# A pair-update block on one Trainium2 core: where the second layer norm's statistics are made, and what the gate of the output stage is made from

## The chip, the cores and the metric

The kernel runs on one core of a Trainium2 chip. The core has a matrix engine (TensorE, "PE" in the profile, with its weight loads shown apart as "PEld"), a vector engine (VectorE, "DVE"), an activation engine (ScalarE, "ACT"), a general engine (GpSimd, "POOL"), and an engine that here only issues transfers (SyncE, "SP"). The engines work through their own instruction queues in order and wait for one another by semaphores. Data moves between the main memory and the on-chip memory (SBUF) by 16 DMA engines; TensorE writes its products to a second on-chip memory (PSUM). All data is 32-bit floating point.

The metric is the device time of one execution in microseconds. Unless it is said otherwise, a time below is from one profiled execution.

## The reference

The input x is an image of 256 by 256 positions with 128 channels. Four layers follow one another, each of the form x = x + f(groupnorm(x)), where the group norm takes its statistics over all positions and over groups of four channels. The change concerns the third layer (a triangle update) and the hand-over to the fourth (a 3 by 3 convolution). Cut to what matters, the third layer computes:

```python
pair_norm = layer_norm(groupnorm(x2))                 # over the 128 channels, each position
p = pair_norm @ p_in.T ;  g = sigmoid(pair_norm @ g_in.T)
left, right = g[..., :H] * p[..., :H], g[..., H:] * p[..., H:]
out = einsum('bikd,bjkd->bijd', left, right / 256)    # for each channel d a product of 256 x 256 matrices
out = layer_norm(out)                                 # the second norm, over the 128 channels again
out = out @ p_out.T
gate = sigmoid(pair_norm @ g_out.T)
x3 = x2 + gate * out
```

The fourth layer begins with groupnorm(x3), so it needs the sum and the sum of squares of x3 for each channel before it can start.

## The kernel before, in words

The four layers run one after another. Between them the image lies in main memory, channel by channel: x2T, x3T, znT (the first norm's output) and prodD (the 128 products) are arrays of 128 channels by 65536 positions. The third layer is the method `triangle`, and has three stages.

**First stage** (lines 1198 to 1285, the loop with an order of steps written out by hand). It works through 32 pieces of 2048 positions. For each it loads x2T (`ld`), takes the mean over channels with small matrix products whose result lies in four groups of 32 partitions (`mn`, `vr`, the helper `four`), spreads such a row back over all partitions with another small product (`spreads`, which gives `mb` and `pr`), forms the reciprocal root `rs` with Ln and Exp on ScalarE, normalises (`zn`), stores the result to znT (`sto`), and makes a quarter of the factors left and right (`fill`). In the list `order`, a pair (step, lag) means that in turn `it` the step works on piece `it - lag`.

**Second stage** (lines 1287 to 1316). The channels are handled in G = 4 groups of CQ = 32. For each group after the first, znT is read again (tile `zt`, in a ring of five buffers, loaded by SP) and the factors of the group are made (tile `z` in PSUM, 64 blocks, a sigmoid on ScalarE and a multiplication on VectorE into the tile `LR`). Then follow 32 channels: four products into `po` in PSUM, two copies by ScalarE that scale and reorder it into `o` (a ring of three), and a store to prodD that GpSimd issues.

**Third stage** (lines 1322 to 1414, called the output stage below). Again 32 pieces of 2048 positions, two halves of 1024 each. `load` fetches prodD, znT and x2T on SP's queue. `mean` and `centre` subtract the mean over channels from the product, `root` makes the reciprocal root of the variance (with a change of ScalarE's table), `scale` applies it, `gates` makes sigmoid(we * znT), `output` makes the last product `py`, multiplies with the gate on VectorE and adds x2 on GpSimd. `stats` then takes the statistics of x3 on VectorE (bn_stats), and GpSimd issues the store to x3T. After 28 pieces `early_statistics` sums up what there is so far. The order is that of the loop's lines; all of it is pinned to the program's order with `pin`.

After the third stage the method `convolution` calls `group_affine`, which reads the statistics (`mean_variance`), and begins with its products `m`.

Most instructions are issued through helpers, so that the profile gives the helper's line: L61 is every matrix product, L55 every ScalarE activation, L1136 is the line that wraps matrix, VectorE and GpSimd instructions of `triangle`. They are told apart by the names of their tiles.

Of the kernel before, what the change touches and what calls it, by code (L numbers as in the profile page):

```python
# [17 lines left out]
P = 128  # L18
# [13 lines left out]
class Kernel:  # L32
# [78 lines left out]
    def mean_variance(self, pool, stats, tag, shift):  # L111

        nc = self.nc
        mv = pool.tile([P, 2], F32, name=f"mv{tag}")
        if shift is None:

            e, e8 = self.early[tag]
            last, dd = (pool.tile([P, 2], F32, name=f"{n}{tag}") for n in ("ml", "md"))
            nc.vector.bn_aggr(last, stats[:, NCH * 7 // 8:])
            nc.vector.scalar_tensor_tensor(mv, last, 0.125, e8, ALU.mult, ALU.add)  # L120
            nc.vector.tensor_tensor(dd[:, 0:1], e[:, 0:1], last[:, 0:1], ALU.subtract)
            nc.vector.scalar_tensor_tensor(dd[:, 1:2], dd[:, 0:1], 7 / 64, dd[:, 0:1], ALU.mult, ALU.mult)
            nc.vector.tensor_tensor(mv[:, 1:2], mv[:, 1:2], dd[:, 1:2], ALU.add)
        else:

            nc.vector.tensor_reduce(mv, stats, AX.X, ALU.add)
            nc.vector.tensor_scalar_mul(mv, mv, 1.0 / NPIX)
            e = pool.tile([P, 2], F32, name=f"me{tag}")
            nc.vector.tensor_tensor(e[:, 0:1], mv[:, 0:1], shift, ALU.add)
            nc.vector.tensor_tensor(e[:, 1:2], e[:, 0:1], e[:, 0:1], ALU.mult)  # L130
            nc.vector.tensor_tensor(mv[:, 1:2], mv[:, 1:2], e[:, 1:2], ALU.subtract)
        return mv

    def early_statistics(self, stats, tag):

        nc, pin = self.nc, self.tc.keep_in_program_order
        e, e8 = self.early[tag]
        pin(nc.vector.bn_aggr(e, stats[:, :NCH * 7 // 8]))
        pin(nc.vector.tensor_scalar_mul(e8, e, 0.875))
# [989 lines left out]
    def triangle(self, x2T, x3T, znT, prodD, stats2, shift2, stats3, prepare):  # L1129
# [12 lines left out]
        with ExitStack() as c:  # L1142
            wp = c.enter_context(self.pool(name="tw", bufs=1))
            with self.pool(name="twp", bufs=2, space=PSUM) as ps0:
                ab = self.group_affine(wp, ps0, stats2, self.g4, "2", shift=shift2, busy=11)
# [12 lines left out]
                V.tensor_scalar_mul(wo, oraw, low)  # L1158
# [8 lines left out]
            zp = quarters.enter_context(self.pool(name="tz", bufs=5))  # L1167
# [27 lines left out]
            with ExitStack() as c1:  # L1195

                LR = c1.enter_context(self.pool(name="tl", bufs=1)).tile([P, 2, 2, 2 * CQ, P], F32, name="LR")
                with ExitStack() as c2:
# [20 lines left out]
                    def ld(d):  # L1219
                        d["x"] = zp.tile([P, 2048], F32, name="zn", tag="zt")  # L1220
                        nc.sync.dma_start(d["x"], x2T[:, d["p"] * 2048:(d["p"] + 1) * 2048])
# [25 lines left out]
                    def pr(d): d["pr"] = spreads(ps, d["rs"])  # L1247

# [10 lines left out]
                    def fill(k):  # L1259
# [17 lines left out]
                     (ld, 0), (mn, 0), (pr, 2), (zn, 2), (af, 2), (f3, 3), (f1, 3), (mc, 0), (s3, 3), (t3, 3),  # L1277
# [12 lines left out]
                table(SIGMOID)  # L1290
                for g in range(G):

                    for b in range(NB if g else 0):
                        if b % 2 == 0:
                            zt = zp.tile([P, 2048], F32, name="zt", tag="zt")
                            nc.sync.dma_start(zt, znT[:, b * 1024:(b + 2) * 1024])
                        z = ps.tile([P, 8, P], F32, name="z", bufs=3)
# [9 lines left out]
                    for d in range(CQ):  # L1307
                        po = ps.tile([P, 2, 2, P], F32, name="po")
                        for a in range(2):
                            for kc in range(2):  # L1310
                                mm(po[:, a], LR[:, a, kc, d, :], LR[:, :, kc, CQ + d, :], start=kc == 0, stop=kc == 1)
                        o = io.tile([P, 2, P, 2], F32, name="o")
                        for a in range(2):
                            act(o[:, a], po[:, a].rearrange("p b j -> p j b"), AF.Copy, scale=1.0 / N)
                        nc.gpsimd.dma_start(prodD[g * CQ + d].rearrange("(p a j) -> p a j", p=P, a=2),  # L1315
                                            o.rearrange("p a j b -> p a (j b)"))

# [4 lines left out]
            with ExitStack() as c1:  # L1322
                io = c1.enter_context(self.pool(name="t3", bufs=3))
                work = c1.enter_context(self.pool(name="t3w", bufs=2))
# [372 lines left out]
```

## Time and profile before

| What | Value |
|---|---|
| time before, median of 3 runs | 4766.66 us (4765.46 to 4775.34) |
| the profiled execution's own time | 4772.24 us |
| its span, first to last instruction | 4770.2 us |
| mean granted TensorE clock in it | 0.992 of full speed |
| TensorE busy over the span | 4587.0 us, 96% |
| VectorE, ScalarE, GpSimd busy | 3641.1, 3390.9, 2012.0 us |
| DMA packets moved | 801.67 MB, mean 168 GB/s |

The table is to be read with care: busy shares are means over four layers with different limits. Every duration that is used below comes from the profiled execution, whose own time is 5.6 us above the median of the runs. The stages of the third layer are told apart in it by time from the span's start: the first stage up to about 3270 us, the second up to 3841, the output stage up to about 4241, then the convolution.

### The profile page before, as it was taken

The page shows a single profiled execution, that of the slowest core. Times are in us where ns is not written, and L with a number is a line of the kernel's source. Part 1 is how long each engine was busy: PE and PEld are TensorE (multiplying, and loading weights), DVE is VectorE, ACT ScalarE, POOL GpSimd, SP SyncE. Part 2 cuts the span into 40 slices and gives each one's busy share as a digit, 9 for nine tenths or more (in the row PEclk, how much of TensorE's full clock was granted, in tenths as well). Part 3 has the DMA queues.
Part 4 walks back from the last instruction along what each step waited for, and adds up shares of the span by engine and source line. Part 5 has one row for each costly group of instructions (what it writes and reads, how often), then busy time and mean ns, then how long its engine had stood idle before and what let it go on. Part 6 is the DMA issues. An engine that isn't in the chain of part 4 may idle for free.

```text
span 4770.2 us, 79683 instructions
## 1 busy us (share of the span) xinstructions
PE 4587.0 (96%) x30927; PEld 2608.0 (55%) x30927; DVE 3641.1 (76%) x4617; ACT 3390.9 (71%) x5135; POOL 2012.0 (42%) x1356
## 2 busy tenths in 40 slices
PE   8999999999999999999999997899999999999999
PEld 2444555555555433333333332557999943369999
DVE  6776777777777699999999998783533458899886
ACT  6555888888888799999999998895333367742110
POOL 0343555555555456676766666332011024420000
PEclk9999999999999999999999999999999999999999
DMA  8893122222222245555555554665866689954332
GB/s 303 302 347 135 46 89 84 81 86 84 85 81 89 77 94 134 132 132 131 135 132 131 134 132 109 243 257 213 280 241 223 224 311 385 367 211 166 127 121 72
DMA packets 216568, 801.67 MB, mean 168 GB/s; under 512 B 58646, under 2 KB 61996, under 8 KB 171748
## 3 DMA queue, kind: packets, MB, share of 16 engines
q1 hardware_dynamic: 140014, 464.64, 29.1%
q0 software_dynamic: 74880, 331.50, 23.4%
q8 instruction: 248, 4.06, 0.4%
q14 instruction: 130, 1.06, 0.1%
q10 hardware_dynamic: 1296, 0.40, 0.0%
HBM read 464.29 MB, written 265.03 MB: 153 GB/s over the span
## 4 chain that ended last, share of the span: by engine, by line
PE 65%; ACT 14%; DVE 10%; issue 6%; DMA 2%; POOL 2%; SPq 0%; ACTq 0%; POOLq 0%; DVEq 0%
PE z L61 10%; PE m L61 8%; PE nd L61 7%; PE sc L61 6%; PE po L61 5%; PE pr L61 3%; PE ppq L61 3%; PE ppv L61 3%; PE zc L61 2%; PE pe L61 2%; PE py L61 2%; PE ppg L61 2%; PE ppk L61 2%; PE px L61 2%; ACT L950 2%
## 5 line engine op out<-in xcount | busy, mean ns | idle before, releaser
L609 DVE TENSOR_TENSOR e<-sc,bT 128x1024 f32<-128x1024 f32 x512 | 613.5, 1219 | 255.6 <-PE sc L61 253.5
L609 POOL TENSOR_TENSOR ks<-e 128x1024 f32<-128x1024 f32 x256 | 602.0, 2370 | 442.3 <-PE nd L61 428.9
L55 ACT ACTIVATE e<-e 128x1024 f32<-128x1024 f32 x512 | 539.3, 1053 | 39.5 <-DVE e L609 29.9
L1136 DVE TENSOR_TENSOR LR<-z,sg 128x512 f32<-128x512 f32 (+1 forms) x320 | 269.4, 873 | 336.3 <-ACT sg L55 336.3
L61 PE MATMUL m<-U,v 128*128 128x128 f32 x4608 | 514.7, 275 | 0.0
L61 PEld LDWEIGHTS m<-U,v 128*128 128x128 f32 x4608 | 514.6, 192 | 0.0
L61 PEld LDWEIGHTS z<-wf,zt 128*128 128x128 f32 x3072 | 343.5, 192 | 0.2
L61 PE MATMUL z<-wf,zt 128*128 128x128 f32 x3072 | 343.5, 275 | 0.0
L55 ACT ACTIVATE sg<-z 128x512 f32<-128x512 f32 (+1 forms) x320 | 160.6, 512 | 244.6 <-PE z L61 244.3
L61 PE MATMUL sc<-proj 32*128 32x256 f32 x4096 | 300.2, 403 | 3.0 <-DVE e L609 2.1
L978 POOL TENSOR_TENSOR fs<-f 128x512 f32<-128x512 f32 x64 | 175.2, 2737 | 270.1 <-DVE f L975 250.6
L1315 POOL DMA_DIRECT2D prodD<-o x128 | 69.3, 542 | 508.8 <-ACT o L55 499.1
L61 PEld LDWEIGHTS sc<-proj 32*128 32x128 f32 x4096 | 188.1, 185 | 160.8 <-PE px L61 94.8
L61 PE MATMUL nd<-e,proj 128*32 128x256 f32 x4096 | 272.3, 383 | 2.6 <-DVE og L609 2.6
L55 ACT ACTIVATE dn<-dn 128x512 f32<-128x512 f32 x384 | 237.9, 619 | 10.3 <-DVE dn L609 6.2
L978 POOL TENSOR_TENSOR u<-t,tr 128x512 f32<-128x512 f32 x64 | 238.2, 3721 | 11.0 <-DVE tr L981 9.7
L1136 POOL TENSOR_TENSOR xin<-ga,xin 128x1024 f32<-128x1024 f32 x62 | 145.6, 2365 | 213.7 <-DVE ga L1136 213.7
L978 POOL TENSOR_TENSOR t<-t,v 128x1024 f32<-128x1024 f32 x64 | 210.1, 3283 | 59.3 <-DVE t L975 59.3
L61 PE MATMUL po<-LR 128*128 128x256 f32 x1024 | 222.3, 380 | 7.2 <-DVE LR L1136 6.3
L1573 ACT COPY m4s<-m 128x512 f32<-128x512 f32 x32 | 18.7, 583 | 287.1 <-PE m L61 287.1
L1583 POOL DMA_DIRECT2D out_dram<-ys x32 | 37.0, 1156 | 423.9 <-DVE ys L1581 423.9
L61 PEld LDWEIGHTS po<-LR 128*128 128x128 f32 x1024 | 194.1, 190 | 34.6 <-DVE LR L1136 7.1
(392 smaller groups left out, 10986.0 us busy)
## 6 DMA issues: line engine op xcount, KB each, us to landing
zt<-znT SPq DMA_DIRECT2D x96, 1024.0 KB
znT<-zn POOLq DMA_DIRECT2D x61, 1024.0 KB, 6.2
xin<-in_x_dram SPq DMA_DIRECT2D x48, 1024.0 KB
xr<-x3T SPq DMA_DIRECT2D x46, 768.0 KB
x1T<-x POOLq DMA_DIRECT2D x64, 512.0 KB, 4.9
xf<-x1T SPq DMA_DIRECT2D x64, 512.0 KB
xc<-x1T SPq DMA_DIRECT2D x128, 256.0 KB
xc<-t POOLq DMA_DIRECT2D x64, 512.0 KB, 4.7
```

The source lines that it names most:

```text
L55: return self.nc.scalar.activation(out, in_, func, bias=bias, scale=scale, **kw)
L61: return self.nc.tensor.matmul(out, lhsT, rhs, start=start, stop=stop)
L609: pin = lambda f: lambda *a, **k: tc.keep_in_program_order(f(*a, **k))
L950: pin(nc.scalar.preload_act_table_set(want))
L978: pin(nc.gpsimd.tensor_tensor(out, a, b_, op))
L1136: pin = lambda f: lambda *a, **k: tc.keep_in_program_order(f(*a, **k))
L1315: nc.gpsimd.dma_start(prodD[g * CQ + d].rearrange("(p a j) -> p a j", p=P, a=2), o.rearrange("p a j b -> p a (j b)"))
L1573: nc.scalar.copy(m4, m[4])
L1583: nc.gpsimd.dma_start(out[row:row + 8].rearrange("r p t c -> p (r t) c"), ys.rearrange("p g k t c -> p (g k t) c"))
```

## The change

The second norm's mean is no longer taken from the data. The output matrix is multiplied with the centring matrix ahead of the loops, which subtracts the mean over channels in the product itself. The second norm's variance is summed up in the second stage: for each channel, VectorE subtracts a shift (the first channel's product) from `po` and adds the difference to `total`; ScalarE squares the difference; GpSimd adds three of four squares to `even`, VectorE the fourth to `odd`. At the end of the stage the reciprocal root is made once, in a tile of 128 x 512, and written to main memory as rs3D, a single row of 65536 values. The first norm's root is written in the first stage to a like row rs2D (step `sr`). The ring of five buffers `zt` becomes five fixed tiles X[0] to X[4]; the factors use four of them, X[4] holds the sums. `po` moves to the ring of `z` tiles in PSUM, which has four instead of three.

In the output stage the rows rs2D and rs3D are read back (`roots`: one partition of each group of 32 holds 512 positions of each of four pieces) and spread over all partitions by a product with a row of ones (`pa`, `pb`). The gate is made from x2: (x2 - mean) times the first norm's root (`xs`), multiplied with a matrix that holds the group norm's scale and the centring (`wec`). znT is no longer read here. The statistics of x3 come from accumulators: the sum from the multiplication with the gate (`gy`), the sum of squares from a square on ScalarE (`qu`). The loop has a written order with lags, and four PSUM tiles of 1024 instead of three and two of 512.

The diff, cut to its core (small weights made ahead of the loops, the convolution's use of the new statistics, and renamings are left out):

```diff
+                    def sr(d):
+                        for k in range(4):
+                            o = d["p"] * 2048 + k * 512
+                            nc.sync.dma_start(rs2D[:, o:o + 512], d["rs"][32 * k:32 * k + 1])
...
-                     (ld, 0), (mn, 0), (pr, 2), ...
+                     (ld, 0), (sr, 2), (mn, 0), (pr, 2), ...
...
+                shift, total, even, odd = (X[4][:, k * 512:(k + 1) * 512] for k in range(4))
+                nc.gpsimd.memset(X[4][:, 512:], 0.0)
+                squared = []
+                def add_square():
+                    if squared:
+                        n, t = squared.pop()
+                        act(t, t, AF.Square)
+                        if n % 4:
+                            pin(nc.gpsimd.tensor_tensor)(even, even, t, ADD)
+                        else:
+                            tt(odd, odd, t, ADD)
...
-                            zt = zp.tile([P, 2048], F32, name="zt", tag="zt")
+                            zt = X[b // 2 % 4]
-                        z = ps.tile([P, 8, P], F32, name="z", bufs=3)
+                        z = ps.tile([P, 8, P], F32, name="z", bufs=4)
...
-                        po = ps.tile([P, 2, 2, P], F32, name="po")
+                        po = ps.tile([P, 8, P], F32, name="z", bufs=4)[:, :4]
...
                         nc.gpsimd.dma_start(prodD[g * CQ + d]...)
+                        add_square()
+                        if g + d == 0:
+                            act(shift, po.rearrange("p k j -> p (k j)"), AF.Copy, scale=1.0 / N)
+                        else:
+                            df = io.tile([P, 512], F32, name="df", bufs=3)
+                            stt(df, po.rearrange("p k j -> p (k j)"), 1.0 / N, shift, MUL, ALU.subtract)
+                            tt(total, total, df, ADD)
+                            squared.append((g * CQ + d, df))
+                add_square()
+                tt(even, even, odd, ADD)
+                stt(total, total, -1.0 / P, total, MUL, MUL)
+                tt(even, even, total, ADD)
+                table(LN_EXP)
+                act(even, even, AF.Ln, bias=self.eps, scale=1.0 / P)
+                rsm = io.tile([P, 2, P, 2], F32, name="o")
+                for a in range(2):
+                    act(rsm[:, a], even[..half a..], AF.Exp, scale=-0.5)
+                nc.sync.dma_start(rs3D[0].rearrange("(p n) -> p n", p=P), rsm...)
...
+                def roots(b, name, src, queue=nc.sync):
+                    if b * 4 < M:
+                        R[name, b] = io.tile([P, 4, 512], F32, name=name)
+                        v = src[0].rearrange("(p k n) -> k p n", k=4, n=512)
+                        for k in range(4):
+                            queue.dma_start(R[name, b][32 * k:32 * k + 1], v[k:k + 1, 4 * b:4 * b + 4])
+                def spread_of(d, name):
+                    b, j = divmod(d["p"], 4)
+                    d[name] = [ps.tile([P, 1024], F32, name=name, tag="w") for _ in range(2)]
+                    for k in range(4):
+                        mm(d[name][k // 2][:, (k % 2) * 512:(k % 2 + 1) * 512], ones[32 * k:32 * k + 1], R[name, b][32 * k:32 * k + 1, j])
+                def lx(d):
+                    if d["p"] % 4 == 0:
+                        roots(d["p"] // 4 + 1, "ra", rs2D)
+                    load_x(d)
+                def lp(d):
+                    if d["p"] % 4 == 2:
+                        roots(d["p"] // 4 + 1, "rb", rs3D)
+                    load_pd(d)
+                def pa(d): spread_of(d, "ra")
+                def xs(d):
+                    d["xs"] = io.tile([P, 2048], F32, name="xs", bufs=2)
+                    for h in range(2):
+                        stt(half(d["xs"], h), half(d["x"], h), shift3, d["ra"][h], ADD, MUL)
+                def e0(d): product(d, "pe", 0, wec, "xs")
+                def e1(d): product(d, "pe", 1, wec, "xs")
+                def sg(d): ...  act(half(d["ga"], h), d["pe", h], AF.Sigmoid, bias=wbe)
+                def pb(d): spread_of(d, "rb")
+                def sc(d): ...  tt(half(d["pd"], h), half(d["pd"], h), d["rb"][h], MUL)
+                def y0(d): product(d, "py", 0, wo, "pd")
+                def y1(d): product(d, "py", 1, wo, "pd")
+                def gy(d): ...  stt(g, d["py", h], wbo, g, ADD, MUL, accum_out=stats3[:, 0, ...])
+                def ad(d): ...  (tt if last piece else gpsimd)(x, ga, x, ADD)
+                def qu(d): ...  act(ga, x, AF.Square, bias=shift3, accum_out=stats3[:, 1, ...])
+                def st(d): pin(nc.gpsimd.dma_start)(x3T[...], d["x"])
+                roots(0, "ra", rs2D)
+                roots(0, "rb", rs3D, nc.gpsimd)
+                order = (
+                     (lx, 0), (pa, 0), (y0, 1), (y1, 1), (xs, 0), (lp, 0), (gy, 1), (e0, 0), (pb, 0), (ad, 1),
+                     (sc, 0), (e1, 0), (sg, 0), (qu, 1), (st, 1),
+                )
```

## The prediction

> **What bounds the kernel now.** I read the table of stretches first, because the page's shares are means over four layers. Its columns are: stretch, length, busy us (x instructions) of PE, PEld, DVE, ACT and POOL, granted clock, DMA share, GB/s. The rows are one round of 32 products, one round of factors, and the steady part of the output stage.
>
> ```profile
> 3442.00:3498.00 56.00, 55.43 (x257) 48.82 (x258) 0.51 (x1) 20.41 (x62) 16.58 (x31) 1.00 0.41 159
> 3498.00:3614.00 116.00, 114.43 (x1025) 114.24 (x1023) 67.01 (x64) 38.87 (x66) 0.76 (x2) 1.00 0.85 287
> 3873.00:4187.00 314.00, 311.18 (x1315) 107.78 (x1314) 256.30 (x271) 235.09 (x249) 142.29 (x81) 1.00 0.97 376
> ```
>
> TensorE is full in all three at full clock. While the products run VectorE does nothing and ScalarE and GpSimd are at a third: that is the room the new sums go into. In the output stage the DMA engines are nearly full too (0.97).
>
> The timeline of the output stage shows one of its turns:
>
> ```profile
> 3884.48 3.70 PE L61 MATMUL pe<-zn,w2e 128*128 128x512 f32 x8
> 3888.11 1.14 PE L61 MATMUL pr<-mr,tspread 32*128 32x512 f32 x8
> 3889.35 3.70 PE L61 MATMUL py<-pr,two 128*128 128x512 f32 x8
> 3892.98 1.14 PE L61 MATMUL pr<-rs,tspread 32*128 32x512 f32 x8
> 3894.05 1.07 PE L61 MATMUL var<-sq,tmean 128*32 128x512 f32 x8
> 3894.94 1.04 PE L61 MATMUL mn<-pr,tmean 128*32 128x512 f32 x8
> 3895.91 3.70 PE L61 MATMUL pe<-zn,w2e 128*128 128x512 f32 x8
> ```
>
> From start to start: pe 3.63, spread 1.24 (1.07 of work, 0.17 of waiting), py 3.63, spread 1.07, var 0.89, mn 0.97, together 11.43 us, and the next turn follows without a gap. A product of 2048 positions costs 3.63, a spread 1.07, because its four small products run side by side in groups of 32 rows.
>
> The chain that ended last gives the ends of the stages:
>
> ```profile
> 3785.77 55.52 PE po L61 x256
> 3841.32 8.14 DMA zn<-znT
> 3849.60 6.48 PE pe L61 x8
> 4246.97 83.08 PE m L61 x744
> ```
>
> A channel's four products take 55.52 / 32 = 1.735 us. The last ends at 3841.3, which I call T. The output stage cannot start before its first load lands (T + 8.3), and the convolution's products start at 4246.97, T + 405.7.
>
> **The change part by part.** *Output stage, a turn.* It loses mn, var and the wait, and keeps pe and py (as e0, e1, y0, y1) and two spreads: 2 x 3.63 + 2 x 1.07 = 9.40 us; I take 9.45. The others must stay below. VectorE: xs 2 x 1.28 and sc 2 x 1.21 (the rows of the zn and pr steps), gy 2 x (1.28 + 0.08; the accumulator's read is 83 ns in the attention) = 7.7. ScalarE: sg 2 x 1.02, qu 2 x (1.15 + 0.19, rows of sq with a bias and of an accumulator's read) = 4.7, with no table load. GpSimd: 2 x 2.36, a store of 0.57 and 0.30 ahead of it = 5.6. DMA: 3 MB instead of 4; 11.43 x 0.97 x 3/4 = 8.3. SP: two loads of 0.32, and on average two of the small root loads. So TensorE still ends last. The written order holds by a hand schedule from pa at 0: xs until 3.7, gy until 6.4, pb's end 7.6, sc until 10.1, and y0 of the next turn wants its data and its PSUM tile at 10.5: the slack is 0.4 us, the thinnest of the turn. If sc were late, y0 would be late by as much.
>
> *Output stage, start.* After T the last channel still has to go through df 0.69, Square 0.62, even 1.30, two VectorE additions of 0.68, Ln 0.69, two Exp 0.66 and some eight hand-overs of 0.1: T + 6.2. The store of rs3D (0.33 to issue, 2.3 to land, the row of prodD<-o) and the read back on GpSimd's queue (four issues of 0.54, 2.3 to land) give rb at T + 13.3. On SP's queue the rs3D store stands in front of everything else: behind it wait eight root loads (8 x 0.33) and the first load of x, which needs about 8.1 as zn did, and whose memory may be X[4]. So the first turn starts between T + 9.7 (x loaded early, only pb waits) and T + 17.6 (x queued behind the store). I take T + 14. *The sum:* first turn, without y0 and y1, 6.1; 31 turns of 9.45, 293; the last y0, y1 3.65; after them gy 1.36, two additions on VectorE 2.46, Square with accumulator 1.34, a reduction and four tiny steps 0.8, hand-overs 0.3, so 6.3 (before: 8.6 from the last py at 4230.05 to the mean at 4238.65); then 8.3 to the convolution as before. 14 + 6.1 + 293 + 3.65 + 6.3 + 8.3 = 331.3 against 405.7: **-74.4 us**.
>
> *Second stage.* Per channel VectorE gets df 0.69 and total 0.68 and every fourth time odd 0.68 (about 0.60 start to start); ScalarE gets a Square of 0.62 beside o 0.66; GpSimd three times in four an addition of 128 x 512 beside its 0.54 store. Taken alone each fits: per four channels (6.94 us) VectorE 6.2, ScalarE 5.3, GpSimd 3 x 1.30 + 4 x 0.54 = 6.1. But these three rows are from engines with a free way to memory. The recurrence's timeline has GpSimd's addition beside VectorE:
>
> ```profile
> 2238.28 1.30 POOL L978 TENSOR_TENSOR t<-fs,ar 128x512 f32<-128x512 f32 x1
> 2244.53 4.48 POOL L978 TENSOR_TENSOR u<-t,tr 128x512 f32<-128x512 f32 x1
> 2244.91 1.22 DVE L975 TENSOR_TENSOR q<-q,ig 128x1024 f32<-128x1024 f32 x1
> 2246.05 0.68 DVE L975 TENSOR_TENSOR u<-u,tr 128x512 f32<-128x512 f32 x1
> 2246.65 1.22 DVE L975 TENSOR_TENSOR yf<-yf,g 128x1024 f32<-128x1024 f32 x1
> 2247.78 1.21 DVE L981 SCALAR_TENSOR_TENSOR v<-q,bx 128x1024 f32<-128x1024 f32 x1
> ```
>
> The same form takes 1.30 or 4.48. The slow one ends at 2249.01, 1.23 after VectorE came to v, the first of the row that reads a PSUM tile (bx) in place of a second SBUF tile. **The Trainium skill, page "SBUF — State Buffer", section "SBUF: two separate sides"**, says of the port pair that the two engines share that it is an exclusive lock: a GpSimd op, or a VectorE op with two SBUF inputs (against a GpSimd op that reads SBUF), has it for the whole instruction, and "the other fully blocks". This speaks against the change, which sets such pairs beside each other. The row of 1.30 alone makes this stage cost nothing; by the rule, total and odd (two SBUF inputs each) and even exclude one another, while df, with po in PSUM, does not. Then four channels go: three times even 1.30 and total 0.60, then total 0.60 left over from the last, odd 0.60, df and hand-over to Square 0.80 more, in all some 7.7 against 6.94. The products are behind by 0.76 per four channels, 6.1 at the end of a round of 32. The four PSUM tiles and the shift of work into the factor rounds (VectorE 58% busy there) hide perhaps half. Bounds: 0, and 93 us if GpSimd's stores are shut out too (4 x 0.54 on top of 7.7 is 9.86, so 2.92 x 32); against that end speaks the recurrence's store xc<-yf, 0.88 at 2229.36 beside a two-input VectorE op of the usual 1.23. I take 3 us a round: **+12**.
>
> Four PSUM tiles instead of three and two, and four zt buffers instead of five, I cost at nothing: a tile of po is given back by df about 1 us after its products, and a zt load has 3 x 3.57 = 10.7 us to land where the load of zn at T needed 8.1; without that cover each of the 96 loads would hold TensorE up by what it is late, perhaps a microsecond.
>
> *First stage.* sr adds four small DMA issues (4 x 0.33) a turn to SP's queue, behind ld and waiting for rs. The next ld, now at 3100.68, stands behind it and goes out at about 3105.1; mn needs it at 3112.7, 7.6 us later, and the store of the same size lands in 5.6 (median). I cost it at 0.5; if the load took 9, a turn would give back 1.4, 45 us in all. rs has one buffer, and its next Ln comes 5 us after sr's issue, 2.3 to land: covered. Weights ahead of the loop (two products of 128 x 128, some ten VectorE steps of 0.16 to 0.28): mostly in idle time around 2992 to 2996, +1.
>
> *Sum:* -74.4 + 12 + 1.5 = -61 us. The profiled execution took 4772.24 us; the median of the runs is 5.6 below, and the stages are as long in it, so 4766.7 - 61 = **4706 us**.
>
> **The rivals.** *Main (0.82):* as above, 4680 to 4745.
>
> *The DMA engines decide (0.06).* They were 0.97 busy at 376 GB/s, and the start of the old stage ran at 289. If the new mix (thin loads of one partition) gets only 300 GB/s, 3.15 MB a turn take 10.5 us: 1.05 x 32 = 34 us given back, 4740. Against it: 419 GB/s were reached at 3862 to 3873.
>
> *The shared port is worse (0.07).* Stores shut out as well, 93 in place of 12: the gain is eaten, 4766 + 20 at the worst, about 4786; half of it gives no change.
>
> *One-row spreads do not run side by side (0.05; slower).* pa and pb contract over one row each at partitions 0, 32, 64, 96. If they went one after another, each would cost 4 x 0.91 = 3.63 in place of 1.07, a turn 14.5, and 32 x 5.1 = 164 us come on top: 4870. It decides from 2.0 us for a spread on: then the turn's gain is gone. Against it: the recurrence's zb contracts over 14 rows, in pairs at two partitions, and its 128 products took 74.6 us, 0.58 each, less than 0.91. For it: the only one-row product of the trace stands at partition 0, alone.
>
> *The change does not do what it says:* the old chain (mean, centre, root, zn) is gone from the loop in the diff, so only the sums' place is in doubt, which is the port's case.
>
> **How the numbers follow.** Range: the main case's ends are 4689 (nothing lost at the port and start at T + 9.7: -74.4 - 4.3 + 1.5 = -77), or 4680 with turns of 9.2, and 4735 (24 at the port, start at T + 17.6, turns of 9.9: -74.4 + 3.6 + 14 + 24 + 1.5 = -31), or 4745 with ten more in the first stage; I let it reach to 4752 for the DMA case and the milder port case. Left out are the one-row case and most of the bad port case, some 0.15. A measurement of this kernel can tell about 0.2% (9.5 us) from no change. Faster by more: main and DMA case and a third of the port case, 0.90; within: 0.03; slower: 0.07.
>
> **What would show it.** Right: turns of 9.4 to 9.5 us in the output stage with TensorE full; pa and pb at 1.07; ScalarE without table loads there; first pa at T + 10 to 18; products of a round at 55.5 to 60 us, additions even at 1.3 to 2.0 us, with VectorE's total stretched where they meet. Wrong: spreads at 3.6, a DMA share of 1.0 with waits on x or pd, rounds of products over 65 us, TensorE waiting for zn loads in the first stage (turns over 8.1).

## The result and the profile after

| What | Before | After |
|---|---|---|
| median of 4 runs each | 4769.91 us | 4735.84 us (4734.19 to 4737.28) |
| ratio, with its 95% interval | | 0.9928 [0.9911, 0.9945] |
| the profiled execution's own time | 4772.24 us | 4734.19 us |
| its span | 4770.2 us | 4732.1 us |

The change makes the kernel faster by 34.1 us in the medians and by 38.05 us in the two profiled executions (4772.24 - 4734.19). The forecast was 61 us. The stages, read from the chain that ended last in both profiles, say where the rest stayed. T' is the end of the last product of the second stage in the profile after, 3863.5, as T was 3841.3 before.

| Part | Before | After | Difference | Forecast |
|---|---|---|---|---|
| up to the first product of the second stage | 3269.75 | 3270.62 | +0.9 | +1.5 |
| second stage, first to last product | 571.6 | 592.9 | +21.4 | +12 |
| last product to the convolution's first product | 405.7 | 345.2 | -60.5 | -74.4 |
| convolution to the end of the span | 523.2 | 523.4 | +0.2 | 0 |

The table of stretches of the kernel after (stretch, length, busy us and instructions of PE, PEld, DVE, ACT and POOL, granted clock, DMA share, GB/s), for a piece of a round of products, a round of factors and the steady output stage:

```profile
3450.00:3510.00 60.00, 55.59 (x260) 47.44 (x258) 52.95 (x67) 35.15 (x90) 46.01 (x53) 1.00 0.34 128
3510.00:3624.00 114.00, 112.80 (x1008) 112.64 (x1008) 69.72 (x70) 39.80 (x68) 3.48 (x4) 1.00 0.87 293
3898.00:4189.00 291.00, 291.00 (x992) 108.48 (x992) 226.43 (x249) 136.73 (x182) 161.27 (x92) 1.00 0.88 335
```

Before, TensorE was busy 55.43 of 56 us in the round of products, and VectorE 0.51. Now VectorE has 52.95 of 60 and GpSimd 46.01, and TensorE is busy 55.59 of 60: the products wait. In the output stage TensorE is busy for all 291 us, and the DMA engines came down from 0.97 to 0.88.

From the chain that ended last (start, us, what):

```profile
3883.99 5.34 DMA x<-x2T
...
3917.76 3.63 PE py L61 x8
...
3927.16 3.63 PE py L61 x8
...
4208.74 372.56 PE m L61 x3336
```

From one py to the next it is 9.40 us, in place of 11.43. Before, the stage's first load went out at once at T; now x goes out at 3883.99, which is T' + 20.5, and the first xs starts 5.4 us after that.

The timeline of the products (start, us, engine, line, operation, out<-in, and in brackets the idle time and what ended it):

```profile
3656.36 7.14 PE L61 MATMUL z<-LR 128*128 128x256 f32 x32 [0.81 <-DVE df L1119]
3657.57 0.69 DVE L1119 TENSOR_TENSOR zt<-zt,df 128x512 f32<-128x512 f32 x1
...
3659.92 1.28 POOL L1119 TENSOR_TENSOR zt<-zt,df 128x512 f32<-128x512 f32 x1
3660.59 1.18 DVE L1119 TENSOR_TENSOR zt<-zt,df 128x512 f32<-128x512 f32 x1
3661.86 0.63 ACT L55 ACTIVATE df<-df 128x512 f32<-128x512 f32 x1 [0.64 <-DVE zt L1119]
3662.52 1.04 DVE L1119 TENSOR_TENSOR zt<-zt,df 128x512 f32<-128x512 f32 x1 [0.76 <-ACT df L55]
3664.31 7.14 PE L61 MATMUL z<-LR 128*128 128x256 f32 x32 [0.80 <-DVE df L1119]
```

Here z<-LR are the products of four channels (they now lie in the ring of z tiles), zt is the memory of the sums, and df is the difference, which Square overwrites. Four channels take 3664.31 - 3656.36 = 7.95 us; TensorE waits 0.8 us in each for VectorE to give a PSUM tile back. Two things are to be seen. VectorE's total takes 0.69 us when it starts ahead of GpSimd's even (3657.57), and 1.18 when it starts inside it (3660.59): it then ends 0.57 after even does. And Square (3661.86) is released by that total, although all it needs is df; VectorE then stands idle for 0.76 ahead of odd (3662.52), until Square is done.

The start of the output stage, from the timeline:

```profile
3874.39 0.72 ACT L55 ACTIVATE zt<-zt,eps 128x512 f32<-128x512 f32 x1
3875.13 1.28 ACT L1119 ACT_TABLE_LOAD   x1
3876.42 1.28 ACT L55 ACT_TABLE_LOAD   x1
3877.71 0.84 ACT L55 ACTIVATE o<-zt 128x256 f32<-128x256 f32 x2
3878.99 4.89 SPq L1375 DMA_DIRECT2D ra<-rs2D  x8
3883.99 0.39 SPq L1393 DMA_DIRECT2D x<-x2T  x1
3889.43 2.47 DVE L1119 SCALAR_TENSOR_TENSOR xs<-x,shift,ra 128x1024 f32<-128x1024 f32 x2 [10.19 <-DMA x<-x2T]
```

Between the Ln and the two Exp of the root stand two loads of ScalarE's table: the one for the sigmoid, which the program asks for ahead of the output stage and which came in before the Exp, and the one that brings the old table back. Then SP issues eight root loads for 4.89 us, and x only behind them.

### The profile page after: what moved, and what is told of

It reads as the page before. It is cut to its first block, busy times and chain, and to the rows that moved or that the text cites. A ratio compares the mean times of both kernels' runs of the same rounds, so it can differ in the third digit from the quotient of the medians.

```text
span 4732.1 us, 79416 instructions
## 1 busy us (share of the span) xinstructions
PE 4533.6 (96%) x30421; PEld 2596.8 (55%) x30421; DVE 3791.8 (80%) x4847; ACT 3332.4 (70%) x5174; POOL 2139.1 (45%) x1457
## 3 DMA queue, kind: packets, MB, share of 16 engines
q1 hardware_dynamic: 136286, 432.10, 27.5%
## 4 chain that ended last, share of the span: by engine, by line
PE 61%; ACT 16%; DVE 12%; issue 7%; DMA 2%; POOL 1%; SPq 0%; ACTq 0%; POOLq 0%; DVEq 0%
PE z L61 10%; PE m L61 8%; PE nd L61 7%; PE sc L61 6%; PE ppq L61 3%; PE ppv L61 3%; PE pe L61 2%; PE zc L61 2%; PE py L61 2%; PE ppg L61 2%; PE ppk L61 2%; PE px L61 2%; ACT L933 2%; PE pr L61 2%; ACT x2q L55 2%
## 5 line engine op out<-in xcount | busy, mean ns | idle before, releaser
L55 ACT ACTIVATE e<-e 128x1024 f32<-128x1024 f32 x512 | 539.0, 1053 | 39.2 <-DVE e L592 29.6
L61 PEld LDWEIGHTS z<-wf,zt 128*128 128x128 f32 x4096 | 462.8, 192 | 55.7 <-DVE LR L1119 27.4
L61 PE MATMUL z<-wf,zt 128*128 128x128 f32 x4096 | 475.5, 277 | 7.2 <-DVE LR L1119 4.9
L61 PE MATMUL z<-LR 128*128 128x256 f32 x1024 | 226.6, 381 | 21.4 <-DVE df L1119 15.1
L61 PEld LDWEIGHTS z<-LR 128*128 128x128 f32 x1024 | 192.5, 190 | 54.7 <-issue 21.0
L1616 ACT COPY m4s<-m 128x512 f32<-128x512 f32 x32 | 18.6, 583 | 287.3 <-PE m L61 287.3
L1119 POOL TENSOR_TENSOR x<-ga,x 128x1024 f32<-128x1024 f32 x62 | 144.6, 2347 | 135.6 <-DVE ga L1119 135.6
```

The lines of the kernel that those rows point to most:

```text
L55: return self.nc.scalar.activation(out, in_, func, bias=bias, scale=scale, **kw)
L61: return self.nc.tensor.matmul(out, lhsT, rhs, start=start, stop=stop)
L1119: pin = lambda f: lambda *a, **k: tc.keep_in_program_order(f(*a, **k))
L1616: nc.scalar.copy(m4, m[4])
```

## The experiments

The theory after this reading: the second stage loses 21 us to two waits, the port that VectorE and GpSimd share, and Square's waiting for total because it writes df in place; the output stage loses its 14 us at its start. The rivals: only one of the two waits counts; the start is set by the backlog of the sums, and goes with it; the DMA engines or the spreads bound the turn.

**a_separate: Square writes a tile of its own.** The port stays as it is.

```diff
-                        n, t = squared.pop()
-                        act(t, t, AF.Square)
+                        n, d0 = squared.pop()
+                        t = io.tile([P, 512], F32, name="sqd", bufs=2)
+                        act(t, d0, AF.Square)
...
-                            df = io.tile([P, 512], F32, name="df", bufs=3)
+                            df = io.tile([P, 512], F32, name="df", bufs=2)
```

> Against the changed kernel (4735.8 us), whose rounds of products go 7.95 us per four channels where the products alone take 6.94. Here the square goes to a tile of its own, so that it waits for df alone and no longer for total, which reads the df it used to overwrite (df has two buffers in place of three). Port theory (total and odd exclude even): the exclusion stays, per four channels 3 x 1.30 + 5 x 0.60 and the hand-overs remain, at least 7.4; gain 0 to 15 us. Rival, the square's wait for total is what stretches the round: 6.94 to 7.2 per four channels, gain 20 to 25 us.

Measured: 4715.98 us, ratio 0.9891 [0.9874, 0.9907], 19.9 us below the kernel after. Four channels take 7.45 us. From its timeline:

```profile
3657.34 1.28 POOL L1119 TENSOR_TENSOR zt<-zt,sqd 128x512 f32<-128x512 f32 x1
3658.03 1.16 DVE L1119 TENSOR_TENSOR zt<-zt,df 128x512 f32<-128x512 f32 x1
3658.09 0.63 ACT L55 ACTIVATE sqd<-df 128x512 f32<-128x512 f32 x1 [0.64 <-DVE df L1119]
```

Square now starts beside total and is released by df. The total is as stretched as before (1.16). So the in-place write was a wait of its own, on top of the port's.

**b_psum_total: total is summed from PSUM**, so that of VectorE's additions only every fourth, odd, reads two SBUF tiles; the 127 shifts are subtracted at the end.

```diff
-                            tt(total, total, df, ADD)
+                            stt(total, po.rearrange("p k j -> p (k j)"), 1.0 / N, total, MUL, ADD)
...
+                stt(total, shift, -127.0, total, MUL, ADD)
                 stt(total, total, -1.0 / P, total, MUL, MUL)
```

> total adds po straight from PSUM (the shift is taken off once at the end), so total has one SBUF input and no longer reads df. Both theories expect the rounds to come back to the products' own 6.94 us per four channels or close to it (gain 18 to 26 us): the port is shared only with odd, once in four, and the square waits for df alone. A third theory, that VectorE, ScalarE and GpSimd are simply too busy together with four PSUM tiles, expects no gain, because as many instructions of the same sizes remain.

Measured: 4713.92 us, ratio 0.9884 [0.9867, 0.9900]. Four channels take 6.94 us: in the chain that ended last the 248 products that close the stage (31 channels) run without a gap,

```profile
3787.59 53.81 PE z L61 x248
```

and the round's period is 171.60 us as before the change. That the second stage can be had for nothing is shown. The whole times of a and b, 2 us apart, are not told apart; their second stages are (see the table below).

**c_read_only: total from PSUM, but with a column of df as its factor.** This kernel leaves out the right sum of differences (the square of the mean is not subtracted); it keeps Square waiting for total while total has left the port.

```diff
-                            tt(total, total, df, ADD)
+                            stt(total, po.rearrange("p k j -> p (k j)"), df[:, 0:1], total, MUL, ADD)
...
-                stt(total, total, -1.0 / P, total, MUL, MUL)
+                stt(total, total, -1e-30, total, MUL, MUL)
```

> As the run with total from PSUM, but total takes one column of df as its per-partition factor, so that the square, which overwrites df, must still wait for total. This leaves the sum of the differences wrong, and the square of the mean is not subtracted from the variance. Port theory: rounds near 6.94 per four channels, gain 15 to 26 us, as with total from PSUM. Rival (the square's wait for total): the wait is still there, so rounds stay near 7.9, gain under 8 us.

Measured: 4724.92 us, ratio 0.9907 [0.9891, 0.9924]; four channels 7.70 us. In its timeline odd, now the only VectorE addition with two SBUF inputs, is still held up:

```profile
3656.80 1.33 DVE L1119 TENSOR_TENSOR zt<-zt,df 128x512 f32<-128x512 f32 x1 [0.76 <-ACT df L55]
```

The same instruction in b_psum_total takes 0.69. The total itself takes 0.75 where b has 0.68, also when it starts inside even. The four kernels together, with the second stage from first to last product (which repeats: three profiles of kernels with the statistics as in the kernel after have 592.8 to 592.9, seven with those of b have 570.3):

| Kernel | total on the port | Square waits for total | four channels, us | second stage, us | median, us |
|---|---|---|---|---|---|
| after | yes | yes | 7.95 | 592.9 | 4735.84 |
| a_separate | yes | no | 7.45 | 577.6 | 4715.98 |
| c_read_only | no (odd is stretched) | yes | 7.70 | 586.3 | 4724.92 |
| b_psum_total | no | no | 6.94 | 570.3 | 4713.92 |

A round has eight times four channels, and the products take 6.94. The excess in a round is then 8.1 us in the kernel after, 4.1 in a and 6.1 in c, and over four rounds 32, 16 and 24. Against b the second stage rose by 22.6, 7.3 and 16.0. So about 2 us of each round's delay is hidden (the difference, over four rounds, is 8 to 9 us), and what goes beyond is paid. Neither wait alone explains the loss: the port alone costs 7.3 us of the stage, and the in-place write adds 15.3 to it (after against a). The in-place write alone costs at most the 16.0 of c, for c is not free of the port: odd is stretched by 0.64 in each four channels. The two costs nearly add up. The medians, 21.9, 2.1 and 11.0 above b's, also hold differences outside of the stage: b's profile has its first product of the stage 3.3 us later than a's and 2.6 later than c's, and its output stage is 1.8 and 3.9 us longer.

**d_start: the store of rs3D on GpSimd's queue** in place of SP's, to let x out early.

```diff
-                nc.sync.dma_start(rs3D[0].rearrange("(p n) -> p n", p=P), rsm...)
+                nc.gpsimd.dma_start(rs3D[0].rearrange("(p n) -> p n", p=P), rsm...)
```

> The store of rs3D goes out on GpSimd's queue, where its reader waits anyway, in place of SP's, where the root loads and the first load of x stand behind it (issued 20.5 us after the last product, landed 5.3 later). Queue theory: x and ra are loaded while the root is still being made, the first xs starts 5 to 12 us earlier, and the read of rb decides; gain 5 to 12 us. Rival: the first x lies where the sums lie (X[4]) and can't be loaded before the root is done; gain under 3 us.

Measured: 4739.85 us, ratio 0.9936 [0.9919, 0.9952], no gain. From its timeline:

```profile
3879.64 0.33 SPq L1393 DMA_DIRECT2D x<-x2T  x1
3879.91 0.56 POOL L1355 DMA_DIRECT2D rs3D<-o  x1 [6.54 <-ACT o L55]
3893.99 5.57 PE L61 MATMUL rb<-rb,tones 1*128 1x512 f32 x8 [3.88 <-DMA rb<-rs3D]
```

x goes out at 3879.64, just behind the last Exp, which ends at 3879.61: with the store out of its way it still waits for the sums to be done with X[4], whose memory it takes. And the small store, now on GpSimd's queue and issued among the large loads, took 7.08 us to land by the chain of waits, so that rb is late.

**e_double_spread: the spread ra is made twice** into the same tiles in each turn.

> The changed kernel with the spread of the first root (ra) issued twice into the same PSUM tiles, four products more a turn of the output stage. TensorE theory: a turn is its products and nothing else, so each grows by one spread, 1.07 us, from 9.40 to 10.47, and the run by 31 to 35 us (about 4769). Rival, the DMA engines or the order of the waits set the turn: it stays near 9.4 to 9.8 and the run grows by under 15 us. If one-row spreads did not run side by side, the turn would grow by 3.6.

Measured: 4763.34 us, ratio 0.9989 [0.9979, 0.9998], 27.5 us above the kernel after. A turn takes 10.26 us, 0.86 more, and 32 x 0.86 = 27.5. The stretch of its output stage:

```profile
3900.00:4180.00 280.00, 280.00 (x1078) 106.32 (x1076) 195.35 (x214) 118.27 (x158) 138.46 (x79) 0.98 0.85 318
```

TensorE is full (the 0.98 is the start, where the granted clock was 0.50 until 3909.7), and what is added to it is paid in full: it bounds the turn. The second set of four products costs 0.86 and not 3.6, so the one-row products do run side by side.

**f_gate_znT: b, with the gate from znT as before the change**, 4 MB loaded and stored in a turn in place of 3, no xs and no spread ra.

```diff
+                load_zn = load("zn", znT, 4)
...
-                def e0(d): product(d, "pe", 0, wec, "xs")
+                def e0(d): product(d, "pe", 0, we, "zn")
...
-                     (lx, 0), (pa, 0), (y0, 1), (y1, 1), (xs, 0), (lp, 0), ...
+                     (lz, 0), (lx, 0), (y0, 1), (y1, 1), (lp, 0), ...
```

> The statistics as in the run with total from PSUM, but the gate made as before from znT (loaded again, 4 MB a turn), without the spread of the first root and without xs. The products of a turn come to 2 x 3.63 + 1.07 = 8.33 us. If TensorE alone decided, the run would be about 34 us faster than the run with total from PSUM (4714). DMA theory: 4 MB took 11.43 x 0.97 = 11.1 us of the DMA engines before, so a turn stays at 10.8 to 11.3 us and the run is 40 to 60 us slower than that one, about 4760: the gate from x2 is what lets the shorter products count.

Measured: 4720.79 us, ratio 0.9901 [0.9881, 0.9921]; its interval overlaps that of b. Its stretch, and two rows of its waits in the same time (what waits, for what: us in total, times, longest):

```profile
3900.00:4180.00 280.00, 239.96 (x675) 91.56 (x676) 139.32 (x170) 121.66 (x171) 146.32 (x84) 0.98 1.01 424
```

```profile
PE py L61 <- DVE pd L1119: 38.5, 24, 2.3
DVE pd L1119 <- DMA pd<-prodD: 94.9, 28, 4.3
```

The loads bind now: TensorE has 40 us of idle time in 280, and VectorE's sc in its turn waits for pd to land. The kind is as expected, the size is not: I had read 0.97 at 376 GB/s as nearly full, and here the same engines move 424. A turn is 10.0 us in the mean, and the stage from the first py to m 326.2 us against 309.7 in b; the start without xs gives 6 us back (first py at 29.6 us after the last product, in b 35.6). So what the change gains in its output stage is the mean and variance that left TensorE; making the gate from x2 is worth some 7 to 10 us of it.

**g_start2: b, and three edits at the start of the output stage.** The sums move to X[3] (whose memory x does not take first), the store of rs3D goes on ScalarE's queue, and the table load for the sigmoid that came ahead of the Exp is dropped.

```diff
-                shift, total, even, odd = (X[4][:, k * 512:(k + 1) * 512] for k in range(4))
+                shift, total, even, odd = (X[3][:, k * 512:(k + 1) * 512] for k in range(4))
...
-                            zt = X[b // 2 % 4]
+                            zt = (X[0], X[1], X[2], X[4])[b // 2 % 4]
...
-                nc.sync.dma_start(rs3D[0]...)
+                nc.scalar.dma_start(rs3D[0]...)
...
-                table(SIGMOID)
```

> On top of total from PSUM (4713.9): the sums lie in X[3] in place of X[4], which is under the third buffer set (rb) and not under the first x; the rs3D store goes out on ScalarE's queue; the explicit load of the sigmoid table ahead of the output stage is dropped. Placement theory: x(0), x(1) and ra are in place before the root is made, Ln and Exp lose two table loads of 1.28, and the first xs starts 8 to 14 us earlier after the last product (it was 22 us); rb's store and read back decide; gain 6 to 12 us. Rival: the read back of rb ends as late as the loads did, since the loads of x and pd now crowd its way (7.1 us for the store in the run with GpSimd's queue); gain under 4 us.

Measured: 4705.75 us, ratio 0.9868 [0.9852, 0.9885], 8.2 us below b. The stage from last product to m takes 337.3 us, in b 345.4. Of these 8.1 us, 5.7 are x (the first xs starts 18.3 us after the last product, in b 24.0); the other 2.4 are the granted clock, of which more below: it came back 3.9 us after the first pe, in b 8.7. x is still not early: it goes out at 3857.88 behind the last of the eight root loads (3857.23), which starts just as the store of rs3D has landed (3855.19 + 2.02).

**h_best: g, 20 filler products in place of 26 ahead of the convolution, and two buffers for rs in the first stage.**

```diff
-                        d["rs"] = work.tile([P, 512], F32, name="rs")
+                        d["rs"] = work.tile([P, 512], F32, name="rs", bufs=2)
...
-                ab, mg, sd = self.group_affine(..., shift=shift3, busy=26)
+                ab, mg, sd = self.group_affine(..., shift=shift3, busy=20)
```

> The run with the new placement, and two small things more: 20 in place of 26 filler products ahead of the convolution's statistics (the product pm waited 1.3 us for them), and two buffers for the first stage's root, so that Ln never waits for the store of rs2D (waits of 1.5 and 4.9 us in all). Expected 1 to 5 us below the run with the new placement alone. Rival: the filler's end is not the last wait and the first stage's waits were hidden; under 1 us.

Measured: 4703.78 us, ratio 0.9864 [0.9848, 0.9881]: not told apart from g. The small product pm, which in the kernel after stood 1.3 us behind the mean until the fillers were done, now follows the mean (4172.40) at 4172.52. From last product to m it is 341.5 us, more than in g: in g the clock came back at about 3868.8, 3.9 us after the first pe, here 15 us after it.

**i_x_first: h, with x issued ahead of the root loads of the next pieces.**

```diff
                 def lx(d):
+                    load_x(d)
                     if d["p"] % 4 == 0:
                         roots(d["p"] // 4 + 1, "ra", rs2D)
-                    load_x(d)
```

> Edit against h_best: at the top of the output stage's load step, x is issued ahead of the four root loads of the next pieces instead of behind them. In h_best x went out at 3852.52 because the last of those root loads, in front of it on SP's queue, waited for the store of rs3D to land. Theory A (x waits only for its place in the queue): x goes out at least 5 us earlier, before the sums are done, and then the store of rs3D and the reading of its row set the start: the first xs comes earlier but the first sc and so the second turn wait for rb; 2 to 6 us gained, about 4700. Theory B (x's memory or its queue is held by something else, such as the o tiles or X): x is issued at about the same time and nothing is gained, 4704 as before; the four root loads only come later. Theory C (the early loads of x and pd delay the small store, as when that store went on GpSimd's queue): rb is later by 3 us or more and the time is 4704 to 4708.

Measured: 4708.53 us, ratio 0.9873 [0.9857, 0.9890], no gain. The first xs now starts 12.8 us after the last product instead of 18.4, as theory A said, but the store and the reading back of rb do not come earlier: rb has landed 20.9 us after the last product (its load took 6.74 among the large ones), and the stage takes 343.3 us against 341.5. The clock had a part in this too: it was back at 1.00 at 3858.7, but fell again at 3862.1, while TensorE waited for rb, and stayed at 0.50 until 3875.8. The second half of pe shows it:

```profile
3863.94 3.78 PE L61 MATMUL pe<-xs,twe 128*128 128x512 f32 x4
```

What x first would gain at full clock was not tried.

**j_filler and k_filler28: filler products in the gap before the first pe.** In h_best, as in the kernels after, b and g, the first pe took 3.78 us in place of 1.88, and the column of granted clock says why (the 0.50 behind the five engines' busy times; here h_best):

```profile
3859.00:3874.00 15.00, 14.65 (x28) 4.90 (x29) 6.32 (x6) 2.23 (x2) 0.00 (x0) 0.50 1.01 304
```

```diff
                 def pa(d):
                     spread_of(d, "ra")
+                    if d["p"] == 0:
+                        t = ps.tile([P, 1024], F32, name="busy", tag="w")
+                        for _ in range(74):      # k_filler28: 28
+                            mm(t[:, :P], self.ident, self.cmat)
```

> Edit against h_best: 74 small filler products (128x128, 0.117 us each at full clock, together 8.7) are put behind the first spread ra of the output stage, into the gap of 9.4 us in which TensorE waits for the first xs. In h_best the granted clock there was 0.50 from about 3851 to 3874, and the first products took twice their time (pe x4 3.78 in place of 1.88, rb x8 2.09 in place of 1.14). Theory A (the clock falls because TensorE is idle, and the half clock costs time): the clock stays at or near 1.00 through the gap, pe x4 takes 1.9, the spreads 1.1, and the first turns are 5 to 7 us shorter in all; about 4697 to 4699. Theory B (in these turns the loads of x and pd decide, with the DMA engines at 0.97 to 1.07 until 3877, and the half clock is hidden behind them): the clock stays up, but TensorE then waits for x or pd, and the time is 4702 to 4704, as before. Theory C (the fillers are late or slow): if the clock falls all the same they take up to 17 us instead of 8.7 and push the first pe back by up to 8; about 4710.

Measured with 74: 4714.36 us, ratio 0.9869 [0.9848, 0.9890]. I had counted one instruction for a filler; in 32 bits each is two, so the fillers took 18.7 us and held the first pe back by 10 us. That is theory C. But the first pe after them took 1.88 us at full clock, and the second py came only 2.3 us later after the last product than in h_best (3889.74 - 3845.02 against 3881.97 - 3839.60), which pointed to the smaller number.

> Edit against h_best: 28 filler products in place of the 74 of the run before. A filler of 32-bit data runs as two instructions of 0.117 us, so the 74 took 18.7 us and held the first pe back by 10 us behind its xs; yet the second py came only 0.7 us later after the last channel's product than in h_best (44.8 against 44.1 us). 28 of them are 56 instructions: about 3.4 us at half clock and 4.9 at full, done when the first xs is. Theory A (the half clock is what h_best loses there): the first pe starts within 1 us of its xs at a granted clock of 1.00 and the turns follow at once; the second py comes at about 37 to 39 us after the last channel's product, 5 to 7 us gained, ratio to before about 0.985. Theory B (rb or the loads of x and pd decide, as when x was issued first): TensorE waits for sc or x in the first two turns, the second py comes at 42 to 44 us and the ratio stays at 0.9864.

Measured with 28: 4701.77 us (4700.88 to 4704.76), ratio 0.9856 [0.9839, 0.9872]. First the two kernels' timelines of TensorE, h_best, then k_filler28:

```profile
3859.35 3.78 PE L61 MATMUL pe<-xs,twe 128*128 128x512 f32 x4 [9.44 <-DVE xs L1119]
```

```profile
3852.96 8.15 PE L61 MATMUL busy<-cmat,ident 128*128 128x128 f32 x56
3862.76 1.95 PE L61 MATMUL pe<-xs,twe 128*128 128x512 f32 x4 [1.65 <-DVE xs L1119]
```

and the stretch of k_filler28 that answers to the one above:

```profile
3862.00:3877.00 15.00, 14.23 (x48) 5.27 (x48) 10.64 (x12) 3.34 (x3) 3.93 (x2) 1.00 1.00 292
```

The first xs starts 18.4 us after the last product in both. With the clock at 1.00 the second py follows 35.3 us after the last product, in h_best 42.4 (3881.97 - 3839.60; the 44.1 of the expectation was counted from the end of the chain's last link, 1.7 too early), and the stage from last product to m takes 334.0 in place of 341.5. So the half clock is shown to be a cost of 7 us in that execution of h_best. It is not the same in each: in g's profile, with the clock back early, the second py follows 36.9 us after the last product, 1.6 later than in k_filler28. The whole time's intervals of h and k still overlap. k_filler28 has the lowest median of all, and is faster than the kernel after: 0.9856 against 0.9928, with intervals far apart. It carries b's and g's edits as well as the fillers.

## Why the prediction was right or wrong, point by point

The time lies in the forecast's range, near its slow end; no error helped another: both large terms, the output stage and the second stage, were forecast too well, by 13.9 and 9.4 us.

**The turn: right.** 9.40 us measured, 9.45 forecast, TensorE full, spreads of 1.07. From the first py to the end of the last it is 293.9 us, where the forecast had 295.6 (31 turns and the last y0 and y1, less the spread of 1.07 that opens a turn ahead of py).

**The tail: right, up to the fillers.** From the last py to the mean 6.05 us (6.3 forecast). From the mean to m it took 9.87 and not "8.3 to the convolution as before": the old 26 fillers (6.07 us) were sized for a longer tail, and pm stood behind them.

**"Output stage, start ... I take T + 14": the step that failed most.** The first py came at T' + 35.4 where the forecast's 14 + 6.1, with the 1.07 of the spread ahead of py, gives 21.2: 14.2 us late, which is the 13.9 that the stage missed in all. Some 10.7 of it is x: the first xs started at T' + 25.9 (forecast 15.2). The terms of the sum that were mis-sized or missing: the sums ran late (the last even ends at T' + 8.8, the last Exp at T' + 15.0 and not T + 6.2), two table loads of 1.28 stood in front of the Exp, and a root load took 0.61 to issue, not 0.33, so eight took 4.89. That x lay in X[4] was named, but only as a doubt: d_start shows that it alone would have held x until the Exp. The backlog is not the main part: b has none, x goes out only 1.9 us earlier there (18.6 us after the last product), and its stage is as long (345.4 us; there the clock came back later). The other 3.5 us lie between the first xs and the first py: 9.5 us where the 6.1 and the spread leave 6.0. Some 2.3 of it is the clock, at 0.50 until about 3895.3 (pe 3.78 for 1.88, the spread 1.50 for 1.14), and the rest, about 1 us, that pe first waits 1.33 for half of xs, for which the 6.1 has no room. The half clock stood in the prediction's own chain: the first pe of the old stage took 6.48 us where a turn has 3.63 (its granted clock was 0.50 until 3855.2).

**"Second stage ... I take 3 us a round: +12": the right mechanism, a second one missed.** The port's exclusion came as **the Trainium skill, page "SBUF — State Buffer", section "SBUF: two separate sides"**, states it (total 0.69 to 1.18 beside even, ending 0.57 after even's end), and four channels without the in-place wait took 7.45, less than the 7.7 that the sum had; a's stage is 7.3 us longer than b's, where the sum had 12. But the same sum let Square start at the end of df. As Square overwrites df and total still reads it, the wait was for total, that is, for an instruction which the port had just stretched. This raised four channels to 7.95 and the stage by another 15.3, to +21.4 against before. That half of a round's delay would be hidden was a guess; about 2 us of it were, of 4.1 in a and of 8.1 in the kernel after.

**First stage: right as far as it can be told.** +0.9 us against 1.5; but b and f_gate_znT, with the same first stage, reach the second at 3272.78 and 3270.70, so one profile does not tell these apart. A store of rs2D was not as quick as the sum had it: in the chain that ended last two of them took 5.62 and 4.63 us, and not 2.3, and Ln waited for one three times, 1.5 us in all. Four PSUM tiles and four zt buffers cost nothing visible: b's rounds run without gaps.

**The rivals.** The DMA engines did not decide (0.88; even with 4 MB a turn they gave 424 GB/s). Stores were not shut out of the port: GpSimd's issues stay at 0.56. The one-row spreads ran side by side (1.07, and 0.86 for another set). None of the three came; what came was the main case near its upper end, at 4735.84, inside its 4680 to 4745, with a second wait in it that no case had named.

**The sum.** +0.9 + 21.4 - 60.5 + 0.2 = -38.0, against 1.5 + 12 - 74.4 = -61. In k_filler28 the second stage takes 570.3 us and the output stage 334.0, -1.2 and -71.7 against before: once the start and the clock are mended the output stage comes out near the forecast's -74.4, and the second stage below its +12, since summing from PSUM takes the port's cost away as well.

## What to carry to other kernels

When work is put on idle engines beside a full one, follow each of its instructions to the buffer it overwrites: a write in place makes it wait for every reader, also on an engine that it has nothing to do with. Price such a wait in the stage where it stands: here whole times put the port at 2 us, where the stage shows 7.3. Where one stage hands over to the next, write down the queue in order, with its own measured issue times and table loads, and look at whose memory the first load takes; a mean stage time says nothing of it. And look at the granted clock in the rows of such a hand-over before pricing its products.

## What the runs showed of the hardware that was not expected

- The granted clock changed in steps of 3.41 us. Read in slices of half a microsecond, it fell at 3843.65 in h_best, rose at 3847.06, fell at 3850.47 and rose at 3874.37, seven steps later; in the kernel after it fell at 3867.94 and rose at 3895.25, eight steps later. The first fall came 2.3 us (a_separate) to 4.7 us (before) after TensorE ran dry. The rise came 3.9 us after the first pe in g_start2, 4.5 in the kernel after and 15.0 in h_best, although TensorE was busy for 14.65 of the 15 us there. **The Trainium skill, page "TensorE: Matmul & The Clock Gate", section "Part 1: The HAM clock gate (the "warmup" mystery)"**, has half rate after an idle window of about 3.4 us and full rate after about 3.4 us of sustained work. The length of the step agrees; the fall after 2.3 us and the 15 us of h_best do not. In h_best the rise ended the first step that held no one-row spread (py from 3870.95 on); the three steps before, as busy, held 0.96 to 2.02 us of spreads each. Whether such products count for less was not tried.
- A DMA busy share of 0.97 was not yet the limit: 376 GB/s stood beside it before, and 424 beside 1.01 in f_gate_znT.
- A set of four one-row products of 512 columns right behind a like one costs 0.86 us, the first 1.07.
- The small store of rs3D landed in 2.02 us on ScalarE's queue and quiet DMA engines (g_start2), and in 7.08 on GpSimd's queue among large loads (d_start). Which of the two differences did it was not tried.
